# Half images at both ends of a gather-fed middle stage, and layer 3's first operands loaded during the gathers

## The chip, the core and the metric

The kernel runs on one core of one Trainium2 chip. The metric is the device time of one execution in microseconds (us). The core has five engines that run side by side, each in its own order: TensorE (PE; matmuls into PSUM, with the loading of weights shown apart as PEld), VectorE (DVE), ScalarE (ACT), GpSimd (POOL) and SyncE (SP, which starts most DMAs).

## The reference

Four layers are applied in turn to `x`, 8 images of 256 channels and 32 x 32 pixels. Layer 0 is an attention block and an MLP (256 to 1024 to 256, relu6), each after a batch norm over all images. Layer 1 is a bottleneck with a deformable 3 x 3 convolution, layer 2 a convolution of signs by signs with a batch norm over all images, layer 3 a second deformable block. What matters here, shortened:

```python
# end of layer 0
h = _relu6(jnp.einsum('bcn,hc->bhn', y2, w1) + bb1[None, :, None])
m = jnp.einsum('bhn,oh->bon', h, w2) + bb2[None, :, None]
xf = xf + m
# layer 1
h = jax.nn.relu(_bn(_conv1x1(x, w1), ...))            # 256 -> 64 channels
off = conv3x3(h, woff) + boff                          # 27 channels
o, mask = off[:, :18], jax.nn.sigmoid(off[:, 18:])     # 9 offsets (y, x) and 9 masks
samp = _bilinear(h, o_y + base_y, o_x + base_x) * mask # 4 cells around each place
h = einsum('bckhw,ock->bohw', samp, w2) + dcn_b
h = jax.nn.relu(_bn(h, ...))
x = jax.nn.relu(_bn(_conv1x1(h, w3), ...) + x)         # 64 -> 256 channels
# layer 2
y = conv3x3(sign(x), sign(weights)) * mean(abs(weights))
yn = (y - mean over all images) * rsqrt(var + EPS) * gamma + beta
x = yn + x
# layer 3
h = silu(bn(conv3x3(x, w_cv1)))                        # 256 -> 128 channels
...
```

The batch norm of layer 2 needs every image's convolution, so layer 3 can't begin before the last one is done.

## The kernel before

`x` lies in SBUF for the whole run: 128 partitions, 2 channel tiles `t`, 8 images `b`, 1024 pixels. A half image `h` is 512 pixels (16 rows), which is one bank of PSUM.

There are three stages. The first is layer 0's attention, to about 2706 us. The middle stage does the MLP of layer 0, layer 1 and layer 2, to about 3559 us; layer 3 follows. Only the middle stage and the first microseconds of layer 3 are changed.

The order of the middle stage comes from a planner, `Order` (L99 to L156). Every step is a "piece" with a key, an engine, a planned duration, a rank, the pieces it comes after, and the buffers that it takes and gives back: `pm` (2 banks) for the MLP, `po` (1), `pl` (3) for everything small, `pc` (1) for layer 2's convolutions; in SBUF `g` (3 gathered tiles), `idx`, `wts` and others. The planner puts next the piece that can start first by its plan, the lower rank first where two start together. It works when the program is built. The orders on PE, ACT, DVE and POOL are then fixed, and each engine runs its own strictly in order, whatever the real durations are.

An image goes through these pieces:

- MLP: `hidden` (L752), `relu6` (L757 on ACT, L759 on DVE), `mlp_out` (L765, 16 passes per half image and tile of channels), `mlp_add` (L769).
- `reduced` (L814) makes 64 channels; the two halves lie in the two halves of the partitions, so their matmuls can run paired. `reduced_relu` (L821) writes them twice into the bordered `h1`, as they are and shifted by one pixel.
- `table` (L827) transposes `h1` into 9 chunks of 128 cells; `table_copy` (L833) and `table_write` (L840, L842) put them into HBM as a table whose rows hold the four corner cells of a place, 8 DMAs of 1.15 MB in all. These are the DMAs of SP.
- `offsets` (L850) is the 3 x 3 convolution that makes offsets and masks, `offsets_copy` (L857) brings it to SBUF, `places` (L864) transposes it, `places_mask` (L872) is the sigmoid, `places_cells` adds the grid (L877) and calls `corners` (L776 to L797): it makes the cells (L791), then the four weights with the mask (L795, L797); L880 makes the index.
- `gather` (L885): 9 indirect DMAs per 128 pixels, 72 per image, all started by POOL. `near_weights` (L894) and `sample` (L907, L911, on DVE) weigh and add the four corners.
- `turn` (L919, L922), `turn_copy` (L931, L933): the samples are transposed back. `contract` (L942) is the deformable convolution's product, 5 blocks by 2 halves; `contract_relu` (L946), `expand` (L952), `expand_add` (L958), `expand_relu` (L962) end layer 1, and `sign` (L965) writes the bordered signs.
- `convolve` (L972): 18 matmuls in bf16 per image, output tile `o` and half; `convolve_stats` (L979), `convolve_copy` (L983) and a DMA of the result as int16 to `acc_d` in HBM (L984).

The convolutions of image `b` are held back until the places of image `b + 4` (at most the last) are done:

```python
piece(("v", *k), "PE", 3.9, 100 * b + 330, [("x", b, 0), ("x", b, 1), ("p", min(b + 4, B - 1))], convolve, *k, take=[("pc", "pl")[b == B - 1]])
```

After the stage, `batch_norm` (L207 to L221) makes the scale and shift of layer 2. Layer 3 has an `Order` of its own. It begins with DMAs of its weights (L1070 is `wc`, the convolution's), with selection matrices (`spread_rows`, L1155 to L1161, transposed by PE through the `ps` banks), and for each image with `load` (L1165, from `acc_d`), `normed3` (L1170, ACT), `add_normed` (L1174, DVE), `border` (L1177, into `xpad`), `convolve3` (L1182) and `silu` (L1187).

## Time and profile before

| | us |
|---|---|
| median of 3 runs | 4257.02 (4256.65 to 4259.13) |
| the profiled execution's own time | 4256.73 |
| its span | 4254.9 |
| first and last start of a gather (L885) | 2791.43 and 3516.02 |
| one gather on POOL, median of 576 | 0.946 |
| a gather's data, issue to landing, median | 2.7 |
| end of layer 2's last convolution | 3555.43 |
| first convolution of layer 3 (L1182) | 3571.01 |
| PE, DVE, ACT, POOL busy in the span | 3972.3, 3026.9, 1858.0, 3313.3 |

All times in rows are from the start of the span. A line of the timeline is start, duration, engine, source line, operation, output and inputs, how many instructions it joins, and in brackets how long the engine had been idle and what ended that. "x16" of an f32 matmul counts passes: an f32 matmul shows two. A row of a window gives the busy time of each engine in that stretch, the granted clock of TensorE as a share of full speed, and the share of time in which the DMA engines were busy. A row of waits gives the waiting engine and line, what it waited for, the sum, the number and the longest.

### The profile page before, as it was taken

What the parts mean: (1) busy time and instruction counts of PE and PEld (TensorE: products, weight loads), DVE (VectorE), ACT (ScalarE), POOL (GpSimd) and SP (SyncE); (2) the same over time, 40 slices, a digit from 0 to 9 for tenths busy, and PEclk for the clock granted to TensorE, in tenths of its full rate; (3) what the DMA queues carried; (4) which work ended last, traced back from release to release, by engine and by line L of the source; (5) the groups of instructions that cost most, each with busy time, mean ns of one, the idle gap of its engine ahead of it and who ended that gap; (6) DMA issues with size and microseconds to landing.
All of it is one profiled execution on the core that took longest, in us unless ns stands there. A gap on an engine that the chain in (4) does not pass through costs nothing.

```text
span 4254.9 us, 60310 instructions
## 1 busy us (share of the span) xinstructions
PE 3972.3 (93%) x20975; PEld 1542.8 (36%) x20975; DVE 3026.9 (71%) x5147; ACT 1858.0 (44%) x3335; POOL 3313.3 (78%) x2023
## 2 busy tenths in 40 slices
PE   6999999999999999999999999898899978999976
PEld 2333333333333333333333333343343333444432
DVE  6767777777777767777677776567777774777665
ACT  2555545545545555555555555332232324443321
POOL 2888889889898898888888889357777771489767
PEclk8999999999999999999999999999999998999998
DMA  5212212212222222122222121134344442000000
GB/s 174 62 54 57 77 50 63 71 50 65 66 56 69 59 59 73 51 65 68 53 60 74 51 62 48 45 99 115 116 120 121 121 132 72 5 11 15 15 15 21
DMA packets 207225, 283.11 MB, mean 67 GB/s; under 512 B 87216, under 2 KB 117440, under 8 KB 206656
## 3 DMA queue, kind: packets, MB, share of 16 engines
q1 hardware_dynamic: 176352, 195.46, 16.2%
q0 software_dynamic: 28720, 77.90, 6.2%
q10 hardware_dynamic: 1840, 5.81, 0.4%
q8 instruction: 169, 2.77, 0.3%
q14 instruction: 144, 1.18, 0.1%
HBM read 181.07 MB, written 63.82 MB: 58 GB/s over the span
## 4 chain that ended last, share of the span: by engine, by line
PE 72%; DVE 13%; POOL 7%; issue 4%; DMA 3%; ACT 2%; SPq 0%; DVEq 0%; POOLq 0%; ACTq 0%
PE av L460 20%; PE pb L403 12%; PE sc L448 11%; PE pb L386 5%; PE pc L1182 5%; POOL g L885 5%; PE pb L534 3%; PE pa L1366 2%; PE pb L330 2%; PE pm L752 2%; PE po L765 2%; DMA g<-table,idx 2%; DVE pm L407 2%; PE pw L1355 2%; DVE r L491 1%
## 5 line engine op out<-in xcount | busy, mean ns | idle before, releaser
L470 POOL TENSOR_TENSOR esum<-esum,e 128x1024 f32<-128x1024 f32 x762 | 1809.0, 2407 | 55.1 <-ACT e L449 54.7
L407 DVE TENSOR_REDUCE pm<-pb 128x1 f32<-128x512 f32 x2016 | 1356.3, 685 | 656.1 <-PE pb L403 652.0
L449 ACT ACTIVATE e<-sc 128x512 f32<-128x512 f32 x2048 | 1056.5, 603 | 677.0 <-PE sc L448 665.7
L460 PE MATMUL av<-e,v 128*64 128x512 f32 x4096 | 1054.2, 593 | 0.0
L403 PE MATMUL pb<-sk,sq 128*64 128x512 bf16 x4032 | 773.2, 387 | 56.3 <-DVE x L542 23.5
L885 POOL DMA_INDIRECT g<-table,idx x576 | 550.4, 955 | 256.4 <-issue 159.0
L403 PEld LDWEIGHTS <-sq 128*64 128x64 bf16 x4032 | 266.7, 109 | 911.5 <-issue 887.0
L448 PE MATMUL sc<-q,k 32*128 32x512 f32 x4096 | 590.6, 641 | 0.0
L468 POOL TENSOR_TENSOR esum<-e 128x1024 f32<-128x1024 f32 x127 | 303.2, 2409 | 298.9 <-ACT e L449 298.9
L460 PEld LDWEIGHTS av<-e,v 128*64 128x64 f32 x4096 | 295.0, 137 | 208.1 <-issue 117.3
L1374 POOL TENSOR_TENSOR part<-part,pr 128x512 f32<-128x512 f32 x224 | 289.4, 1293 | 67.5 <-DVE pr L1360 56.2
L1360 DVE TENSOR_TENSOR pr<-pw,v 128x512 f32<-128x512 f32 x400 | 258.0, 683 | 105.7 <-PE pw L1355 61.3
L1182 PE MATMUL pc<-xpad,wc 128*128 128x512 f32 x576 | 279.0, 611 | 4.1 <-ACT h L1187 4.1
L448 PEld LDWEIGHTS sc<-q,k 32*128 32x128 f32 x4096 | 164.6, 183 | 229.8 <-issue 185.6
L534 PE MATMUL pb<-o,wp 128*64 128x512 f32 x1024 | 244.3, 596 | 1.4 <-DVE r L512 1.2
L752 PE MATMUL pm<-y,wide 128*128 128x512 f32 x512 | 237.9, 609 | 6.1 <-DVE y L726 5.7
L386 PE MATMUL pb<-wide,y 128*64 128x256 f32 x2048 | 241.8, 379 | 0.0
L765 PE MATMUL po<-hid,w 128*128 128x512 f32 x512 | 239.7, 615 | 1.8 <-DVE x L769 1.7
L491 DVE RECIPROCAL r<-r 128x128 f32<-128x128 f32 x252 | 237.1, 942 | 0.1
L390 ACT COPY v<-pb 128x512 f32<-128x512 f32 x128 | 74.9, 585 | 266.0 <-PE pb L386 266.0
L907 DVE TENSOR_TENSOR near_p<-g,near_p 128x320 f32<-128x320 f32 (+1 forms) x384 | 177.3, 462 | 13.2
L911 DVE TENSOR_TENSOR samp<-samp,near_p 128x320 f32<-128x320 f32 (+1 forms) x384 | 174.0, 453 | 13.2
(256 smaller groups left out, 3893.7 us busy)
## 6 DMA issues: line engine op xcount, KB each, us to landing
sq<-lev_d SPq DMA_DIRECT2D x512, 64.0 KB
r<-r SPq DMA_DIRECT2D x504, 64.0 KB
sk<-lev_d SPq DMA_DIRECT2D x496, 64.0 KB
lev_d<-lev SPq DMA_DIRECT2D x180, 128.0 KB
u_d<-u SPq DMA_DIRECT2D x60, 256.0 KB
g<-table,idx POOLq DMA_INDIRECT x576, 2.7
table<-v SPq DMA_DIRECT2D x32, 256.0 KB
out<-res SPq DMA_DIRECT2D x32, 256.0 KB
```

The costliest lines, as they stand in the source:

```text
L386: nc.tensor.matmul(ps[c * 64 : (c + 1) * 64, (mt % 2) * 256 : (mt % 2 + 1) * 256], ys[b][:, t, k0 : k0 + 64], wv[:, t, g * 256 : (g + 1) * ...
L403: nc.tensor.matmul(ps[c * 64 : (c + 1) * 64, :], sq[pair][:, c, q0 : q0 + 64], sk[pair][:, c, kh * HALF : (kh + 1) * HALF], start=True, st ...
L407: nc.vector.tensor_reduce(maxima[m][:, pair, qt, kh : kh + 1], ps, AX.X, ALU.max)
L448: nc.tensor.matmul(ps, k[r, kt * P : (kt + 1) * P], q[r, h * HALF : (h + 1) * HALF], start=True, stop=True)
L449: nc.scalar.activation(es[m, kt, j // 2][:, j % 2, :], ps, AF.Exp)
L460: nc.tensor.matmul(av[i * HD : (i + 1) * HD, :], vss[b, g][:, kt, j * HD : (j + 1) * HD], e[:, i, :], start=kt == 0, stop=kt == NT - 1,)
L470: eng.tensor_add(sums[m, pair], sums[m, pair], es.pop((m, kt, pair)))
L534: nc.tensor.matmul(ps[c * 64 : (c + 1) * 64, :], wp[:, 2 * g + i, o0 : o0 + 64], outs[(b, g, h), i], start=i == 0, stop=i == 1,)
L752: nc.tensor.matmul(ps, w1[:, t, i * P : (i + 1) * P], ys[b, h][:, t, :], start=t == 0, stop=t == 1)
L765: nc.tensor.matmul(pss["o", b, h, t], w2[:, j, t * P : (t + 1) * P], hids[b, h, j], start=j == 0, stop=j == 7)
L885: nc.gpsimd.indirect_dma_start(out=g[:, k, :], out_offset=None, in_=tables[b][:TR, :], in_offset=bass.IndirectOffsetOnAxis(ap=idxs[b][:, t ...
L1182: nc.tensor.matmul(S["c", b, h], wc[:, t, k, :], tap(xpads[t], k, H // 2, h * H // 2), start=t == k == 0, stop=t == 1 and k == 8,)
```

## The change

It does the following things.

1. For image 0, `reduced`, `reduced_relu` and `table` go by half images, the table in chunks 0 to 3 and 4 to 8, and it is written in two parts (8 and 4 DMAs instead of 8 in all). `corners` is split into `cells` and `corner_weights`, for every image: the index no longer comes after the weights, nor the addition of the grid (`places_add`) after the mask. These DVE pieces get a lower rank.
2. For the last image, `contract` to `sign` go by half images, the lower half's contraction in two pieces of 256 columns. `convolve_upper` makes the upper half's convolution in two steps: all that needs the upper half's signs alone (the three lower taps for 15 of the 16 rows), into the MLP's banks `pm`; then the three lower taps of row 15, 12 matmuls of 32 columns. Convolutions of images 3 to 6 wait for the last hidden layer's outputs instead of the last image's places.
3. `w2` moves into a buffer `kept` that outlives the stage. When the last `mlp_out` is done, layer 3's weights `wc` are loaded into the same bytes. Image 0's convolution result is loaded into the bytes of `w1` that hold the first input tile (`ac0`). Layer 3 plans the load of image 0 at zero time.
4. The two `size` tiles of layer 2's weights go into one buffer that is later `h2`, and `scale` has an earlier rank.

The program's second branch for layer 3, for offsets out of range, is adapted to 1 and 3; the trace before shows no instruction of that branch. The diff, cut to its core:

```diff
+    keep = ctx.enter_context(tc.tile_pool(name="keep", bufs=1))
+    kept = keep.tile([P, 18 * P], F32, name="kept")
+    wc = kept.rearrange("p (t k o) -> p t k o", t=2, k=9)
+    ac0 = wide[:, 0, :].bitcast(I16).rearrange("p (t n) -> p t n", t=2)
...
-        w2 = w.tile([P, 8, C], F32, name="w2")
+        w2 = kept[:, 0 : 8 * C].rearrange("p (t o) -> p t o", o=C)
...
-        def corners(pool, wpool, pos, mask, npts, order):
+        def cells(pool, pos, npts, order):
...
+            iy, ix = order
+            cell = pool.tile([P, NT, npts], F32, name="cell")
+            nc.vector.scalar_tensor_tensor(cell, low[:, :, :, iy], float(PW), low[:, :, :, ix], ALU.mult, ALU.add)
+            return cell, low, over
+
+        def corner_weights(pool, wpool, pos, low, over, mask, npts, order):
+
             hi = over
...
-            return cell, wts
+            return wts
...
+        def reduced(b, hs=(0, 1)):
+            if hs[0] == 0:
+                pss["r", b] = bank()
+            ps = pss["r", b]
             for t in range(2):
-                for h in range(2):
+                for h in hs:
...
+        def chunks(b, i):
+
+            m = 8 if b else 4
+            return (0, m) if i == 0 else (m, NCH)
...
+            c0, c1_ = chunks(b, i)
+            for c in range(c0, c1_):
...
+        def table_write(b, c0, c1_):
+
+            if c0 == 0:
+                tables[b] = dram.tile([NCH * P, 4 * CB], F32, name=f"table1_{b}")
...
+                if c0 == 0:
+                    nc.sync.dma_start(tables[b][0 : P - shift, cols], vs[b][shift:P, 0, :])
+                c = max(c0, 1)
+                body = tables[b][c * P - shift : c1_ * P - shift, cols]
+                nc.sync.dma_start(body.rearrange("(t p) c -> p t c", p=P), vs[b][:, c:c1_, :])
...
+        def places_add(b):
+            pos = pss["pos", b] = one.tile([P, NT, K2, 2], F32, name="pos")
             for i in range(2):
                 nc.vector.tensor_add(pos[:, i::2], turned(b, i)[:, :, 0:18].rearrange("p q (k i) -> p q k i", i=2), grid[:, i::2])
-            cell, wtss[b] = corners(one, sb, pos, pss.pop(("m", b)), K2, (0, 1))
+
+        def places_cells(b):
+            cell, low, over = cells(one, pss["pos", b], K2, (0, 1))
             idxs[b] = sb.tile([P, NT, K2], I32, name="idx")
             nc.vector.tensor_scalar_add(idxs[b], cell, float(PW + 1))
...
+        def places_weights(b):
+            wtss[b] = corner_weights(one, sb, pss.pop(("pos", b)), *pss.pop(("l", b)), pss.pop(("m", b)), K2, (0, 1))
...
+        def contract(b, hs=(0, 1), n0=0, n1=HALF):
+            st, st8 = sts[b]
...
+                    v = st[:, i, h * HALF + n0 : h * HALF + n1] if i < 4 else st8[r, n0:n1]
+                    nc.tensor.matmul(ps[h * CB : (h + 1) * CB, n0:n1], wd[r, i, :], v, start=i == 0, stop=i == 4)
...
+        def convolve_upper(b, o, rest):
+
+            if not rest:
+                pss["v", b, o, 0] = pm.tile([P, HALF], F32, name="pm")
+            rows = H // 2
+            taps = [(t, k) for t in range(2) for k in (range(6, 9) if rest else range(9))]
+            for n, (t, k) in enumerate(taps):
+                r0, r1 = (rows - 1, rows) if rest else (0, rows - (k > 5))
+                nc.tensor.matmul(
+                    pss["v", b, o, 0][:, r0 * W : r1 * W], ws[:, t, k, o * P : (o + 1) * P], tap(xbs[b % 2][:, t, :], k, r1 - r0, r0),
+                    start=bool(n == 0 and not rest), stop=bool(rest and n == len(taps) - 1),
+                )
...
-        piece("scale", "PE", 1.0, 300, [("w", 0, 5), ("w", 1, 5)], scale_signs)
+        piece("scale", "PE", 1.0, 60, [("w", 0, 5), ("w", 1, 5)], scale_signs)
...
+            if b == 0:
+                for h in range(2):
+                    piece(("d", 0, h), "PE", 1.72, r, [("a", 0, h, t) for t in range(2)], reduced, 0, (h,), take=["pl"] * (1 - h))
+                    for i in range(2):
+                        piece(("dr", 0, i, h), "ACT", 0.8, r + i, [("d", 0, h), ("dr", 0, i - 1, h)], reduced_relu, 0, i, (h,), give=["pl"] * (h * i))
+                ready = [[("dr", 0, 0, 0)], [("dr", 0, 0, 1)]], [("dr", 0, 1, 0), ("dr", 0, 1, 1)]
+            else:
+                piece(("d", b), "PE", 2.0, r, [("a", b, h, t) for t, h in halves], reduced, b, take=["pl"])
+                piece(("d", b, 0), "ACT", 1.6, r, [("d", b), *old], reduced_relu, b, 0)
+                piece(("d", b, 1), "ACT", 1.6, r + 1, [("d", b, 0)], reduced_relu, b, 1, give=["pl"])
+                ready = [[("d", b, 0)]] * 2, [("d", b, 1)]
...
-                piece(("t", b, i), "PE", (0.9, 0.15)[i], r + 2, [("d", b, 0)], table, b, i, take=["pl"])
-                piece(("tc", b, i), "ACT", (0.6, 0.22)[i], r + 2, [("t", b, i), ("tw", b - 1), ("tc", b, i - 1)], table_copy, b, i, give=["pl"])
-            piece(("tw", b), "SP", 4.0, r, [("tc", b, 0), ("tc", b, 1)], table_write, b, lag=3.0)
-            piece(("f", b), "PE", 4.3, r + 3, [("d", b, 1)], offsets, b, take=["pl"])
+                piece(("t", b, i), "PE", ((0.9, 0.15) if b else (0.4, 0.5))[i], r + 2, ready[0][i], table, b, i, take=["pl"])
+                tw = [("tw", b - 1, 0), ("tw", b - 1, 1)]
+                piece(("tc", b, i), "ACT", (0.6, 0.22)[i], r + 2, [("t", b, i), *tw, ("tc", b, i - 1)], table_copy, b, i, give=["pl"])
+            if b == 0:
+                for i in range(2):
+                    piece(("tw", b, i), "SP", (4.0, 2.0)[i], r, [("tc", b, i)], table_write, b, *chunks(b, i), lag=3.0)
+            else:
+                piece(("tw", b, 1), "SP", 4.0, r, [("tc", b, 0), ("tc", b, 1)], table_write, b, 0, NCH, lag=3.0)
+            piece(("f", b), "PE", 3.2, r + 3 - 2 * (b == 0), ready[1], offsets, b, take=["pl"])
...
+            piece(("pa", b), "DVE", 0.75, r - 400, [("p", b), ("pw", b - 1)], places_add, b)
+            piece(("pm", b), "ACT", 0.5, r, [("pa", b)], places_mask, b, give=["pl"])
+            piece(("pc", b), "DVE", 2.3, r - 400, [("pa", b)], places_cells, b, take=["idx"])
+            piece(("pw", b), "DVE", 2.3, r - 400, [("pc", b), ("pm", b)], places_weights, b, take=["wts"])
...
+            if b == B - 1:
+                break
+            piece(("k", b), "PE", 4.4, -400, [("uc", b, u, j) for u in range(4) for j in range(3)], contract, b, take=["pl"])
+            piece(("kr", b), "ACT", 0.8, -400, [("k", b), ("e", b - 1, 0), ("e", b - 1, 1), "scale"], contract_relu, b, give=["pl"])
             for t in range(2):
                 piece(("e", b, t), "PE", 1.2, -400, [("kr", b)], expand, b, t, take=["pl"] * 2)
                 piece(("ea", b, t), "DVE", 1.45, -300, [("e", b, t)], expand_add, b, t, give=["pl"] * 2)
                 piece(("er", b, t), "ACT", 1.15, -300, [("ea", b, t)], expand_relu, b, t)
-        for b in range(B):
+        b = B - 1
+        for h in range(2):
+            for i, us in enumerate(((2,), (3,)) if h else ((0, 1),)):
+                n0, n1 = (256 * i, 256 * i + 256) if h else (0, HALF)
+                after = [("uc", b, u, j) for u in us for j in range(3)] + ([("k", b, 0, 0)] if h else []) + ([("k", b, 1, 0)] if i else [])
+                piece(("k", b, h, i), "PE", 2.2 if h else 4.4, -400, after, contract, b, (h,), n0, n1, take=["pl"] * (1 - i))
+            piece(("kr", b, h), "ACT", 0.7, -400, [("k", b, h, h), ("e", b - 1, 0), ("e", b - 1, 1)], contract_relu, b, (h,), give=["pl"])
+            for t in range(2):
+                piece(("e", b, t, h), "PE", 0.86, -400, [("kr", b, h)], expand, b, t, (h,), take=["pl"])
+                piece(("ea", b, t, h), "DVE", 0.73, -300, [("e", b, t, h)], expand_add, b, t, (h,), give=["pl"])
+                piece(("er", b, t, h), "ACT", 0.6, -300, [("ea", b, t, h)], expand_relu, b, t, (h,))
+                piece(("x", b, t, h), "ACT", 0.6, -100, [("er", b, t, h)] + [("v", b - 2, o, h_) for o in range(2) for h_ in range(2)], sign, b, t, (h,))
+
+        for b in range(B - 1):
             for t in range(2):
                 piece(("x", b, t), "ACT", 1.05, -100, [("er", b, t)] + [("v", b - 2, o, h) for o, h in halves], sign, b, t)
             for o, h in halves:
                 k = b, o, h
-                piece(("v", *k), "PE", 3.9, 100 * b + 330, [("x", b, 0), ("x", b, 1), ("p", min(b + 4, B - 1))], convolve, *k, take=[("pc", "pl")[b == B - 1]])
+                piece(("v", *k), "PE", 3.9, 100 * b + 330, [("x", b, 0), ("x", b, 1), ("p", b + 4) if b < 3 else ("o", B - 1, 1, 1, 1)], convolve, *k, take=["pc"])
                 piece(("vs", *k), "DVE", 0.7, -500, [("v", *k)], convolve_stats, *k)
-                piece(("vc", *k), "ACT", 0.6, -300, [("vs", *k)], convolve_copy, *k, take=["ac"], give=[("pc", "pl")[b == B - 1]])
+                piece(("vc", *k), "ACT", 0.6, -300, [("vs", *k)], convolve_copy, *k, take=["ac"], give=["pc"])
                 piece(("vd", *k), "SP", 0.4, 0, [("vc", *k)], lambda: None, give=["ac"])
+        b = B - 1
+        for o in range(2):
+            piece(("vu", o), "PE", 3.9, 100 * b + 330, [("x", b, 0, 0), ("x", b, 1, 0), ("h", b, 1, 7)], convolve_upper, b, o, 0, take=["pm"])
+        for h in range(2):
+            for o in range(2):
+                k = b, o, h
+                r = -200 + 10 * h + o
+                if h:
+                    piece(("v", *k), "PE", 3.9, r, [("x", b, 0, 1), ("x", b, 1, 1), ("v", b, 1, 0)], convolve, *k, take=["pl"])
+                else:
+                    piece(("v", *k), "PE", 0.5, r, [("x", b, 0, 1), ("x", b, 1, 1), ("vu", o)], convolve_upper, b, o, 1)
+                piece(("vs", *k), "DVE", 0.7, -500, [("v", *k)], convolve_stats, *k)
+                piece(("vc", *k), "ACT", 0.6, -300, [("vs", *k)], convolve_copy, *k, take=["ac"], give=["pl" if h else "pm"])
+                piece(("vd", *k), "SP", 0.4, 0, [("vc", *k)], lambda: None, give=["ac"])
+
+        piece("wc", "SP", 0.5, 0, [("o", B - 1, 1, t, 1) for t in range(2)], nc.sync.dma_start, wc, d["l3_wcv1"].rearrange("(t p) k o -> p t k o", p=P))
+        piece("ac0", "SP", 0.5, 0, [("h", B - 1, 1, 7)] + [("vd", 0, o, h) for o, h in halves], nc.sync.dma_start, ac0, acc_d[0])
...
+            if b == 0:
+                S["ac", b, t] = ac0[:, t, :]
+                return
...
-                piece(("ld", b, t), "SP", 0.5, r, [], load, b, t, take=["ld"], lag=5.0)
+                piece(("ld", b, t), "SP", 0.5 if b else 0.0, r, [], load, b, t, take=["ld"], lag=5.0 if b else 0.0)
```

## The prediction

> **What bounds the kernel now.** I read the page first (TensorE busy 93% of the span, GpSimd 78%), then the stretch 2706 to 3640 us by windows, since the edits lie only there.
>
> Busy time by window: window, sum, then PE, PEld, DVE, ACT, POOL, the granted TensorE clock, DMA share and GB/s.
> ```profile
> 3336.00:3427.00 91.00, 77.11 (x295) 33.39 (x294) 67.59 (x155) 24.84 (x48) 69.04 (x73) 0.94 0.43 124
> 3427.00:3517.00 90.00, 67.45 (x282) 28.29 (x281) 61.66 (x130) 20.06 (x37) 68.06 (x72) 0.91 0.41 123
> 3517.00:3571.00 54.00, 36.68 (x152) 14.87 (x151) 22.69 (x77) 15.96 (x22) 8.03 (x8) 0.89 0.21 68
> 3571.00:3640.00 69.00, 65.65 (x166) 28.74 (x166) 38.52 (x57) 40.70 (x54) 0.00 (x0) 0.94 0.14 45
> ```
> The first two rows are gathering images: GpSimd starts 72 gathers in each, no engine is full. The waits of GpSimd from 2780 to 3530 say what paces it:
> ```profile
> POOL g L885 <- issue: 159.0, 522, 0.3
> POOL g L885 <- DVE hid L759: 81.5, 2, 81.2
> ```
> A gather takes 0.95 us and the next follows 0.30 later, 576 of them from 2791.43 to 3516.97, with no stall over 0.3 us after the first (which had idled 81.2). So here the time is: when the first gather starts, a fixed 725.5 us, and what follows the last. Work on other engines is free as long as the stream is fed. Rows three and four are what follows: the tail of layers 1 and 2, and layer 3's start, where TensorE is the bound again (65.65 of 69 us).
>
> The timeline before the first gather (start, duration, engine, line):
> ```profile
> 2764.09 7.13 PE L765 MATMUL po<-hid,w 128*128 128x512 f32 x16 [0.84 <-DVE x L769]
> 2772.88 1.94 PE L814 MATMUL pl<-x,c 128*64 128x512 f32 x8
> 2774.95 3.16 ACT L821 ACTIVATE h<-pl,twice 64x512 f32<-64x512 f32 x4 [1.28 <-PE pl L814]
> 2784.68 1.28 ACT L872 ACT_TABLE_LOAD   x1
> 2786.30 0.37 DVE L877 TENSOR_TENSOR pos<-pl,grid 128x72 f32<-128x72 f32 x2 [1.18 <-ACT mask L872]
> 2790.39 0.19 DVE L880 TENSOR_SCALAR idx<-cell 128x72 int32<-128x72 f32 x1
> 2791.43 1.07 POOL L885 DMA_INDIRECT g<-table,idx  x1 [81.21 <-DVE hid L759]
> ```
> It is one chain; the positions wait for the mask's table load, the indices for all weights. The timeline after the last gather:
> ```profile
> 3524.57 4.17 PE L972 MATMUL pc<-xb,ws 128*128 128x512 bf16 x18 [0.80 <-ACT ac L983]
> 3528.66 4.66 PE L942 MATMUL pl<-st,wd 128*64 128x512 f32 x20
> 3533.40 0.78 ACT L946 ACTIVATE h<-pl,twice 128x512 f32<-128x512 f32 x1 [3.26 <-PE pl L942]
> 3539.13 16.30 PE L972 MATMUL pl<-xb,ws 128*128 128x512 bf16 x72 [1.81 <-ACT xb L965]
> ...
> 3571.01 2.05 PE L1182 MATMUL pc<-xpad,wc 128*128 128x512 f32 x2
> 3573.07 16.08 PE L1182 MATMUL pc<-xpad,wc 128*128 128x512 f32 x34
> ```
> A convolution of another image stands ahead of the last contraction, then all 72 convolution matmuls wait for the last sign. Call G the issue of the last gather (3516.02) and C the end of the last convolution (3555.43): C is G+39.4.
>
> **Part 1, first image.** By halves, TensorE gets half 0's table transposes and reduction ahead of the last MLP output. Unpaired, a half's reduction is four passes at 0.43 us, 1.72 instead of half of 1.94; with four transposes (0.77/9 each, 0.35) it puts 2.07 us on that path, and the last add ends at 2774.1 instead of 2772.0. Only half 1 follows: reduction 1.72, two relus of 0.79 instead of four. The offsets (2.95) then start near 2778.7 instead of 2779.07, and the positions' transposes end near 2783.75 instead of 2784.15. The add of positions no longer waits for table load and mask: about 2783.9 instead of 2786.30, 2.4 gained. The indices leave the weights behind: from add to index 2.65 us instead of 4.28, 1.6 gained. First gather at 2786.55 + 0.85 (end of the index to the gather, as now) = 2787.4 against 2791.43: **4.0 us**. The weights (1.5 us, L795 and L797) now lie behind the index and beside the first gathers, whose data land 2.7 us after issue.
> The table is the limit close by. It is written in 12 DMAs instead of 8, the second part four of 160 KB. At the 155 GB/s that the queue ran in 2780 to 2788 this is 4.1 us from 2779.8, and with the landing near 2786, just ahead of the index. The Trainium skill, "DMA: Bandwidth & Descriptors", Anatomy of one DMA, speaks against more DMAs: about 2 us fixed for each. The trace: eight issues spanned 6.1 us and traffic ended 2.6 us after the last. If that stood in series for the four more, 8 us, the table would be there at 2794, part 1 would lose 2.6 and the sum would be 4242.8; in the trace eight lie over each other, so I take the rate. Ends: 2 gained (table late by 2) and 5.
>
> **Gathers, images 1 to 7.** 576 issues stay. The order of instructions puts three 18-matmul convolutions (4.17 each) ahead of the last image's positions on TensorE, whose indices are now ready at 3415.9 for a gather due near 3427.3. Also positions and indices move forward on VectorE relative to the samples: before image 6's index (from 0) the spare time was 1.4 us, now more. For the last image I estimate 3 to 4 us left of 11, with the 4-us earlier start taken off. I book 0, ends 0 and -6 (TensorE's work from the MLP to those positions, all matmuls at their rows' durations, is 642.7 us by the new order and 628.9 by the old; with all 13.8 uncovered, some 6 go beyond the spare time, since the images' other waits take up part).
> The convolution weights of layer 3 (1.18 MB) and its first input add DMA traffic to windows with a DMA share of 0.41: hidden, 0; if the gathers' landings rose by a us, the ring of three buffers covers it. The scale step, index-queue and buffer edits: 0, all inside windows where PE is idle 14 to 22 us of 90. On SP, nothing that a gather needs is queued behind the two new loads once the last table is written.
>
> **Part 2, last image.** After the last sample (G+6.0) come transposes and copies as now. The convolution of 4.17 plus its waits no longer stands before the contraction: it starts near G+7.5 instead of G+12.6, 5.1 gained. Its last piece is 10 passes of 256 columns, half of 4.66: 2.3 gained, less 0.2 for its start. Expand and sign of one half, with 9 to 12 small matmuls before the stats (1.1 to 1.7 us at a weight load of 0.10 to 0.14 each), cost 0.75 more than they save. The 36 upper matmuls, 36 x 0.2264 = 8.15, are taken ahead into TensorE's idle time before G. Together 14.5: C = G+24.9.
> Here the clock weighs against. The rows: this same 18-matmul convolution took 4.17 us after waits of 0.8 to 1.8, but 6.19 at 3489.53 after a transpose that had ended 3.87 us of idleness, and the granted clock fell to 0.50 at 2692 after a gap of 2.49. The Trainium skill, "TensorE: Matmul & The Clock Gate", Part 1, states half rate after about one idle window of 3.4 us, free-running. My tail leaves TensorE idle some 2.6 us (expand ends G+12.7, last sign G+15.3), shorter than the page's window, so by the page no loss (sum 4235.2); by the rows the 36 last matmuls would lose 2.0 (4237.2). The free-running window leaves it open, I take 1: **13.5 us**, ends 10 and 16.
>
> **Part 3, layer 3's start.** With image 0's input resident, the plan puts normalization (L1170, L1174) ahead of most selection pieces (L1159): the first bordered image is ready near C+10.95, the first convolution at C+11.2 instead of C+15.6. 4.4 gained. But six of the ten selection transposes then stand between the convolution's matmuls: 6 x 0.2 to 0.47, less the one there now, 1.4 lost. TensorE starts at half clock both ways: the rows are 2.05 for two passes, then 16.08 for 34, with granted clock 0.50 until 3573 and 0.66 to 3577; the 11-us gap keeps that loss of about 2.3 where it is. By the page it is 3.4 us of half-rate work, 1.7 lost, also in both. **3.0 us**, ends 1 and 6. The load of the weights itself is worth little: issued at 3558.70, it was in before xpad was. The rest of layer 3 has the same order on every engine, with TensorE at 542 of 614 us, so the shift carries to the end.
>
> **Sum.** 4.0 + 0 + 13.5 + 3.0 = 20.5. The profiled execution took 4256.73 (span 4254.9 and 1.8 around it), 0.3 under the median of 4257.02: 4236.2.
>
> **The rivals.**
> 1. A part is lost: the last image's positions stall the gathers by up to 6, or the table is late by 2, or the selection pieces hold the convolution (2 instead of 4.4). For it: 11 us of spare time against 12.5 us of moved matmuls. Against: TensorE idles 14 us in that very window. Loss 6: 4242.
> 2. The clock stays full and layer 3 starts earlier than I think: 16 + 6 + 5 = 27, 4230.
> 3. Slower: VectorE stops. It runs in order, so if the add of the last image's positions stands there waiting for TensorE, the samples behind it wait too, g's three buffers stay full and GpSimd stops. Price: each us beyond the 3.5 spare is one on the gather stream. It decides from 20.5 + 3.5 = 24 us of lateness; at 36, 32.5 are lost against 20.5 gained, 4268.7. Against it: TensorE's moved and added work is 13.8 us, so 36 would need its own waits to grow by 22.
> 4. The change does not do what it says: the tail's gain goes back because the final convolution isn't bound by the last sign (the upper 36 matmuls fall after G instead of before). Price 8.15: 4244. The order shows them all ahead of the last contraction, which is against.
>
> **How the numbers follow.** Forecast 62%, rival 1 21%, rival 2 9%, rival 4 4%, rival 3 4%. Range 4228 to 4246: bounds 27 and 13 of the three parts, with a stall of 3 on the lower. 0.2%, 8.5 us, is what a measurement here can tell from no change. A gain under 8.5 needs two losses at once or half of rival 3: 3%; slower by over 0.2% only rival 3's far end: 2%.
>
> **What would show it.** First gather at 2787 to 2788; no wait over 0.5 us on GpSimd later, above all at 72 gathers from the end; last convolution 25 to 27 us after the last gather, with 36 matmuls in 8.2 (10 if cold); first silu of layer 3 near C+31 instead of C+33.8. The forecast is wrong if a gap stands before the last image's gathers, or if C stays beyond G+30.

## The result, and the profile after

The changed kernel takes 4238.32 us (median of 6 runs, 4236.48 to 4241.13) against 4257.21 (6 runs, 4255.68 to 4259.13): 18.9 us less, a ratio of 0.9955 with a 95% interval of 0.9942 to 0.9968. Forecast were 4236.2, a gain of 20.5, in a range of 4228 to 4246. The profiled execution took 4237.45; its span is 4235.2 against 4254.9, 19.7 less. The new line numbers are `hidden` L758, `mlp_out` L771, `gather` L913, `convolve` L1006, `convolve_upper` L1020, `convolve3` L1277; `places_add` is L899 and the index L904.

The 19.7 us can be followed by five marks in both traces:

| stretch | before | after | gain | forecast |
|---|---|---|---|---|
| span's start to the first gather | 2791.43 | 2788.62 | 2.8 | 4.0 |
| first to last gather | 724.59 | 724.26 | 0.3 | 0 |
| last gather (G) to the end of layer 2's last convolution (C) | 39.41 | 28.97 | 10.4 | 13.5 |
| C to layer 3's first silu table load | 33.80 | 29.25 | 4.6 | 3.0 |
| from there to the end | 665.67 | 664.10 | 1.6 | 0 |

The last row is no effect of the change that these runs could show: it lies anywhere from 664.1 to 665.6 in the kernels below, which all have the same code there.

The waits of GpSimd from 2780 to 3530 after the change (waiting engine and line, releaser, sum, times, longest):

```profile
POOL g L913 <- issue: 159.9, 525, 0.3
POOL g L913 <- DVE wm L806: 79.3, 3, 78.7
```

The stream of gathers has no stall, as before. VectorE's L806 is named for the first gather only because it ended last by the records; the index is what counts. The timeline ahead of that gather (start, duration, engine, line, operation, then idle time and what ended it):

```profile
2767.01 7.13 PE L771 MATMUL po<-hid,kept 128*128 128x512 f32 x16 [0.84 <-DVE x L775]
...
2775.79 1.93 PE L827 MATMUL pl<-x,c 128*64 128x512 f32 x4
...
2785.13 0.37 DVE L899 TENSOR_TENSOR pos<-pl,grid 128x72 f32<-128x72 f32 x2 [4.31 <-PE pl L886]
...
2785.62 1.28 ACT L894 ACT_TABLE_LOAD   x1
...
2787.57 0.20 DVE L904 TENSOR_SCALAR idx<-cell 128x72 int32<-128x72 f32 x1
...
2788.62 1.07 POOL L913 DMA_INDIRECT g<-table,idx  x1 [78.65 <-DVE wm L806]
```

The last MLP output starts 2.9 us later than before (2764.09), the positions no longer wait for the table load, and from their add to the index's end it is 2.6 us. The tail:

```profile
3514.51 0.41 PE L947 MATMUL pl<-ident,samp 128*128 128x128 f32 x2 [1.45 <-DVE samp L939]
...
3518.79 0.69 PE L947 MATMUL pl<-ident,samp 128*128 128x128 f32 x2 [3.87 <-DVE samp L939]
...
3520.16 4.72 PE L972 MATMUL pl<-st,wd 128*64 128x256 f32 x10 [0.25 <-ACT st L959]
3524.91 0.77 ACT L978 ACTIVATE h<-pl,twice 64x512 f32<-64x512 f32 x1 [4.42 <-PE pl L972]
3525.74 3.78 PE L984 MATMUL pl<-h,c 64*128 64x512 f32 x4 [0.86 <-ACT h L978]
...
3531.78 0.40 PE L1020 MATMUL pm<-xb,ws 128*128 128x32 bf16 x9 [1.47 <-ACT xb L999]
3532.02 9.83 PE L1006 MATMUL pl<-xb,ws 128*128 128x512 bf16 x36
```

The reader should see three durations here. Ten contraction passes of 256 columns take 4.72 us, as long as the twenty of 512 columns before, which ran in pairs (4.66). Four expand passes take 3.78, where eight took 3.09. And 36 convolution matmuls take 9.83, where 72 took 16.30. TensorE's windows say why (busy time, PEclk, DMA share, GB/s):

```profile
3509.00:3513.00 4.00, 4.00 (x20) 1.00 0.46 131
3513.00:3516.00 3.00, 0.47 (x3) 1.00 0.32 93
3516.00:3519.00 3.00, 0.21 (x1) 0.91 0.00 0
3519.00:3522.00 3.00, 2.75 (x9) 0.50 0.00 0
3522.00:3525.00 3.00, 2.87 (x7) 0.50 0.00 0
3525.00:3528.00 3.00, 2.26 (x3) 0.50 0.00 0
3528.00:3531.00 3.00, 1.76 (x5) 0.50 0.07 25
3531.00:3534.00 3.00, 2.22 (x14) 0.50 0.70 238
3534.00:3537.00 3.00, 3.00 (x11) 0.75 0.26 87
```

For 17 us the granted clock is half, from 3518.46 to 3535.52. It falls in the 3.87 us in which TensorE waits for the last sample. These 17.07 us are five times 3.41. In all 14 traces shown or named here every spell of half and of full clock lasts a whole multiple of 3.41 us (the last one is cut by the end of the span), so the clock changes from one window of 3.41 us to the next and not at the wait itself. The start of layer 3 has such a spell too (first convolution, first silu's table load, and the stretch between, before and after):

```profile
3553.54 4.04 PE L1277 MATMUL pc<-xpad,kept 128*128 128x512 f32 x6
3571.10 1.28 ACT L1282 ACT_TABLE_LOAD   x1 [0.75 <-PE pc L1277]
```

```profile
3571.01:3589.23 18.22, 18.14 (x38) 0.87 0.29 98
3553.54:3571.10 17.56, 17.56 (x43) 0.93 0.25 76
```

### The profile page after: what moved, and what is told of

Its sections match the earlier page's. It is cut to its first block, busy times and chain, and to the rows that moved or that the text cites. A ratio compares the mean times of both kernels' runs of the same rounds, so it can differ in the third digit from the quotient of the medians.

```text
span 4235.2 us, 60371 instructions
## 1 busy us (share of the span) xinstructions
PE 3972.8 (94%) x20997; PEld 1543.9 (36%) x20997; DVE 3026.4 (71%) x5147; ACT 1862.2 (44%) x3340; POOL 3312.4 (78%) x2023
## 4 chain that ended last, share of the span: by engine, by line
PE 69%; DVE 13%; POOL 8%; issue 5%; DMA 3%; ACT 1%; SPq 0%; DVEq 0%; POOLq 0%; ACTq 0%
PE av L460 20%; PE pb L403 12%; PE sc L448 11%; POOL g L913 6%; PE pb L386 5%; PE pc L1277 5%; PE pb L534 3%; PE pa L1461 2%; DMA g<-table,idx 2%; PE pb L330 2%; DVE pm L407 2%; PE pw L1450 2%; PE pm L758 2%; DVE r L491 1%; PE pb L481 1%
## 5 line engine op out<-in xcount | busy, mean ns | idle before, releaser
L403 PE MATMUL pb<-sk,sq 128*64 128x512 bf16 x4032 | 772.8, 387 | 56.7 <-DVE x L542 23.5
L913 POOL DMA_INDIRECT g<-table,idx x576 | 550.1, 955 | 253.8 <-issue 159.9
L1277 PE MATMUL pc<-xpad,kept 128*128 128x512 f32 x576 | 276.7, 606 | 4.0 <-ACT h L1282 4.0
L758 PE MATMUL pm<-y,wide 128*128 128x512 f32 x512 | 235.6, 606 | 6.1 <-DVE y L732 5.7
L771 PE MATMUL po<-hid,kept 128*128 128x512 f32 x512 | 239.8, 617 | 1.5 <-DVE x L775 1.4
```

The lines of the kernel that those rows point to most:

```text
L403: nc.tensor.matmul(ps[c * 64 : (c + 1) * 64, :], sq[pair][:, c, q0 : q0 + 64], sk[pair][:, c, kh * HALF : (kh + 1) * HALF], start=True, st ...
L758: nc.tensor.matmul(ps, w1[:, t, i * P : (i + 1) * P], ys[b, h][:, t, :], start=t == 0, stop=t == 1)
L913: nc.gpsimd.indirect_dma_start(out=g[:, k, :], out_offset=None, in_=tables[b][:TR, :], in_offset=bass.IndirectOffsetOnAxis(ap=idxs[b][:, t ...
L1277: nc.tensor.matmul(S["c", b, h], wc[:, t, k, :], tap(xpads[t], k, H // 2, h * H // 2), start=t == k == 0, stop=t == 1 and k == 8,)
```

## The experiments

Each kernel is the changed one with the edit shown, but for `before_order`. Totals come with few runs, so most verdicts rest on a stretch of the trace. Where TensorE never waits in a stretch, its work at half clock took twice as long, so half of the time at half clock can be taken off, and what is left compares. The first four kernels ran beside a kernel before of 4258.98; `no_halves` took 4235.54, `scale_later` 4235.80 and `hold_convs` 4238.92, one run each.

**no_halves.** Image 0 is taken whole again.

```diff
-            m = 8 if b else 4
+            m = 8
-            if b == 0:      # reduced, reduced_relu, table_write by halves
+            if b < 0:
```

> The changed kernel, with image 0 taken whole again (reduction, relus, table in 8 DMAs); only the split of index and weights and the add ahead of the mask stay. Theory: the index sets the first gather and the halves bring nothing, since the 2.6 us that they put ahead of the last MLP output eat what they save: first gather near 2787.7, 1 us before the changed kernel's 2788.62. Rival: the table sets it once the index is early; eight DMAs issued to 2786 with traffic to 2788.6, as in the kernel before, then hold the first gather at 2789 to 2790. The prediction's own step (halves worth 0.0 to 0.4 by its terms, 2.07 paid for 2.4 saved) says 2788. Everything behind the first gather shifts with it, within 1 us in the total.

Two lines of the timeline:

```profile
2785.16 0.20 DVE L904 TENSOR_SCALAR idx<-cell 128x72 int32<-128x72 f32 x1
...
2788.46 1.07 POOL L913 DMA_INDIRECT g<-table,idx  x1 [80.13 <-DVE hid L765]
```

The index is there at 2785.36, but the gather starts 3.10 us later instead of 0.85. The last table DMA was issued up to 2784.5 and the DMA engines were busy to about 2786.6; the trace names no other cause, so the table is taken to have held it. The stage had begun 1.64 us earlier in this execution (first hidden matmul 2708.75 instead of 2710.39). Counted from there the first gather comes after 79.71, against 78.23 changed and 80.78 before. In these three the stage began with 5.7, 5.9 and 4.9 us at half clock; with half of that taken off, 76.84, 75.26 and 78.33 are left. The rival is right: the split of index and weights alone earns 1.5, and the halves 1.6 more, all of it through the table, for which the index alone would have been too early.

This kernel shows something else in its tail, where its instructions and their order are the changed kernel's. G to C is 27.09 here, against 28.97:

```profile
3525.13 2.11 PE L984 MATMUL pl<-h,c 64*128 64x512 f32 x4 [0.86 <-ACT h L978]
```

```profile
3523.46:3526.85 3.39, 2.53 (x7) 1.00 0.00 0
```

The clock fell here as well, at 3516.62, but was full for one window of 3.41 us when the expand ran, which took 2.11 instead of 3.78. `scale_later` has the same tail too, and 28.25. A tail without added matmuls so takes 27.1 to 29.0.

**scale_later.** The sum of the weights' sizes is put behind image 0's places.

```diff
-        piece("scale", "PE", 1.0, 60, [("w", 0, 5), ("w", 1, 5)], scale_signs)
+            if b == 0:      # in the loop, behind ("p", 0)
+                piece("scale", "PE", 1.0, 60, [("w", 0, 5), ("w", 1, 5), ("p", 0)], scale_signs)
```

> The changed kernel, with the eight small matmuls that sum the sign weights' sizes (0.8 us of TensorE, ahead of image 0's last MLP output in both kernels) put after image 0's places. Theory (one chain of TensorE sets the first gather): 2788.62 goes to 2787.8. Rival (the table's DMAs are late as well): it stays within 0.3. Nothing else moves; total 0 to 1 us shorter.

The first gather is at 2787.66, 77.53 after the first hidden matmul. But that stage began with 4.6 us at half clock here and 5.9 in the changed kernel's trace; with half of it taken off, 75.23 and 75.26 are left. `warm_tail` and `hold_convs`, whose code is the changed kernel's up to there, have 77.56 and 77.61, both 75.25 without that half. So nothing was gained: the last add did come 0.9 earlier than in those two (62.2 after the stage's start instead of 63.1 and 63.2), but the sum now stood in TensorE's order behind the places, and its result (L753) in VectorE's ahead of the positions' add, which began 1.3 us after the places were begun instead of 0.4. One queue's delay had become another's.

**warm_tail.** Matmuls of constants, read by nobody, fill TensorE's idle time.

```diff
+        def warm(n):
+            ps = po.tile([P, HALF], F32, name="po")
+            for i in range(n):
+                nc.tensor.matmul(ps, ws[:, 0, 0, 0:P], ws[:, 0, 0:2, :].rearrange("p k o -> p (k o)"), start=True, stop=True)
+        piece(("warm", 0), "PE", 0.0, -450, [("u", b, 3, 0), ("vu", 1)], warm, 14)
+        piece(("warm", 1), "PE", 0.0, -450, [("e", b, 1, 1)], warm, 5)
```

> The changed kernel, plus 14 matmuls of constants whose results nobody reads, in TensorE's 3.9 us idle ahead of the last image's last transposes, and 5 more after the last expand. Theory (the tail lost its 4 us against the prediction to the clock, which fell to half in that idle time): the contraction of ten 256-column passes takes 2.4 instead of 4.72, the four expand passes 1.8 instead of 3.78, the last 36 convolution matmuls 8.2 instead of 9.83, and from the last gather's issue to the end of the last convolution it is 23.5 to 25 instead of 29.0; total 4 to 5.5 us shorter than the changed kernel. Rival (the tail waits for ScalarE and VectorE, the clock hides behind it): under 1.5 us. Second rival (work added in TensorE's order is in the way): longer.

G to C is 27.42 instead of the 23.5 to 25 expected, and the median 4235.99 (4 runs; 0.9949, 0.9932 to 0.9965). Only the last 36 matmuls came out at full clock (8.17); contraction and expand were 4.71 and 3.78. The 14 had run too early: the last four transposes are one piece, two of them ready and two waiting for the last sample, and the planner put the 14 ahead of the piece. A gap of 2.63 us was left inside it, and the clock fell in it, at 3516.28. The tail's 27.42 lies within what it takes with no such matmuls, so nothing is shown to be gained.

**hold_convs.** The convolutions of images 3 to 6 wait for the last image's places again.

```diff
-("p", b + 4) if b < 3 else ("o", B - 1, 1, 1, 1)
+("p", min(b + 4, B - 1))
```

> The changed kernel, with the convolutions of images 3 to 6 held back again for the last image's places. Two of them then stand around the last transposes, as in the kernel before. Theory (clock): they keep TensorE at full clock, so the contraction takes 2.4 to 2.6 us and the last 36 matmuls 8.2; but one of 4.2 us stands ahead of the contraction, so the tail from last gather to last convolution is 25 to 29, no longer than the changed kernel's 29.0. Rival (moving them out of the way was worth the predicted 5.1): 32 to 34. For the gathers: no stall before the last image either way; its index is ready some 5 to 12 us earlier than in the changed kernel against the gather.

```profile
3518.43 4.17 PE L1006 MATMUL pc<-xb,ws 128*128 128x512 bf16 x18 [0.61 <-ACT ac L1030]
3522.52 2.51 PE L972 MATMUL pl<-st,wd 128*64 128x256 f32 x10
3525.90 1.98 PE L984 MATMUL pl<-h,c 64*128 64x512 f32 x4 [0.86 <-ACT h L978]
```

The convolution is in the way again and the contraction takes 2.51, the expand 1.98; the clock was full until 3530.22. G to C is 29.12, against 27.1 to 29.0 without the convolutions. Moving them away had bought between nothing and 2 us in the tail, not 5.1: they paid for most of their place by the clock. Of the gathers' spare time: the last image's index was ready at 3407.67, 14.7 us ahead of its first gather (71 gathers of 1.25 before the last); in the changed kernel at 3420.94, 3.2 ahead, and in the kernel before 11.2.

**warm_turn, upper_late, load_planned, before_order** ran on another chip, where the kernel before took 4590.67 us. Between first and last gather single engines stood still there for up to 36 us at a time. A line of ScalarE's timeline in `warm_turn`:

```profile
3501.26 0.78 ACT L980 ACTIVATE h<-pl,twice 128x512 f32<-128x512 f32 x1 [27.44 <-remote]
```

Its input was ready 20 us before (L974 had ended at 3480.91); TensorE had nothing to do from 3483.26 on, but GpSimd went on gathering until 3496.73. So ScalarE stopped first here, and the others ran dry behind it: PE, DVE, ACT and POOL were all idle at once for 6.4 us at most, not up to 28 as the expectation of `warm_turn_2` has it. ScalarE's waits of this kind sum to 335 us in this trace, which is 342 longer than that of `warm_turn_2`. No queue or engine of the profile shows what it waited for, and the gathers stretched to 1025 to 1058 us in all four kernels. Their totals (4575 to 4598), and their tails, say nothing on the change; the start of layer 3 lies behind the stalls and can be read. The two tails were run again.

**load_planned.** `load` for image 0 is planned at 0.5 us and a lag of 5 again; the data are in SBUF as in the changed kernel.

> The changed kernel, with image 0's load planned at 0.5 us and a lag of 5 again, though the data are in SBUF; only the planned order at layer 3's start changes. Theory (the order of normalization against selection pieces is the gain): end of the last convolution to first silu table load goes from 29.25 to 33 to 34, total 4 to 5 longer. Rival (the gain is the data's being there): it stays at 29 to 30.

**before_order.** The kernel before, with this one edit:

```diff
-                piece(("ld", b, t), "SP", 0.5, r, [], load, b, t, take=["ld"], lag=5.0)
+                piece(("ld", b, t), "SP", 0.5 if b else 0.0, r, [], load, b, t, take=["ld"], lag=5.0 if b else 0.0)
```

> The kernel before, with image 0's load planned at zero time and nothing else changed: the load from HBM and layer 3's weights (1.18 MB, issued 3.3 us after the last convolution) stay. Theory (order alone): from the last convolution's end to the first silu table load 29.3 to 30.5 instead of 33.8, total 3 to 4.5 us shorter than the kernel before. Rival (the early order needs the early weights): the first convolution matmul of layer 3, possible near 11.7 us after, waits for the weights, which at the 225 GB/s that the DMA queue reached in short stretches land 9 us after at the earliest and at 155 near 11; silu 31 to 34.

The first silu's table load in `load_planned`, and then in `before_order`; C was 3889.12 and 3878.19:

```profile
3923.91 1.28 ACT L1282 ACT_TABLE_LOAD   x1 [5.20 <-PE pc L1277]
```

```profile
3907.81 1.28 ACT L1187 ACT_TABLE_LOAD   x1 [0.75 <-PE pc L1182]
```

That is 34.79 us after C with the data there and the old plan, and 29.62 with the data and weights loaded as before and the new plan. The order is the gain; the early loads bring nothing that these runs can show. Layer 3's first convolution even started sooner without them: 10.6 us after C in `before_order`, 11.4 to 11.7 with the same order and the early loads, and under the old plan 15.6 before and 16.9 in `load_planned`. What costs this microsecond stays open.

**warm_turn, warm_turn_2.** The 14 matmuls stand inside the last piece of transposes; the five behind the expand stay:

```diff
                     nc.tensor.transpose(ps[:, i * P : (i + 1) * P], sf[:, j, i * P : (i + 1) * P], ident)
+                    if (b, u, j, i) == (B - 1, 3, 1, 1):
+                        warm(14)
```

> The changed kernel, plus 14 matmuls of constants that nobody reads, this time between the second and third of the last image's last four transposes (L947), which is where the 3.9 us of idle TensorE lie; and 5 after the last expand as in warm_tail. There the 14 had run ahead of the first two transposes, an idle gap of 2.6 us was left, and the clock fell at 3516 all the same; only the last 36 matmuls (8.17 instead of 9.83) came out at full clock, 1.55 us gained. Theory (the idle gap sets the clock, the clock the tail): no window at 0.50 from the last gather to the last convolution; contraction 2.5 instead of 4.72, expand 2.0 instead of 3.78; last gather's issue to the end of the last convolution 23.4 to 24.5 instead of 29.0. Rival (the clock falls for low activity, not for one gap): contraction at 4.7 again, 27 or more.

`warm_turn` is one of the four above (4584.69, 0.9993 of a kernel before that stalled alike). The same kernel again:

> The same kernel as warm_turn, which had run on a chip where all engines stood still for up to 28 us at a time in the middle stage (the kernel before took 4590 there), so that its tail could not be read. Expected as there: no clock of 0.50 between last gather and last convolution; contraction 2.5, expand 2.0, last gather's issue to end of last convolution 23.4 to 24.5 instead of 29.0, total 4 to 5.5 us shorter than the changed kernel. Rival (low activity cools it, not one gap): contraction 4.7, 27 or more.

```profile
3512.02 3.19 PE L1030 MATMUL po<-ws 128*128 128x512 bf16 x14
3516.22 0.44 PE L947 MATMUL pl<-ident,samp 128*128 128x128 f32 x2 [1.02 <-DVE samp L939]
...
3517.33 2.51 PE L974 MATMUL pl<-st,wd 128*64 128x256 f32 x10 [0.46 <-ACT st L961]
3520.71 2.17 PE L986 MATMUL pl<-h,c 64*128 64x512 f32 x4 [0.86 <-ACT h L980]
...
3525.61 8.24 PE L1008 MATMUL pl<-xb,ws 128*128 128x512 bf16 x36
```

The gap is 1.02 us, contraction and expand are short again, and G to C is 23.69 instead of 27.1 to 29.0: 3.4 to 5.3 us for work that computes nothing. The median is 4233.02 (4 runs) against a kernel before of 4255.67, 0.9946 (0.9931 to 0.9961). One part of the expectation failed: the clock was at half for one window.

```profile
3518.97:3522.36 3.39, 2.53 (x8) 1.00 0.00 0
3522.38:3525.77 3.39, 3.23 (x19) 0.50 0.51 164
```

In the window ahead of it TensorE had worked for 2.5 of 3.4 us, and its longest gap there was 0.86. So a long gap is not needed; the rival, that low activity brings the clock down, is not refuted by this run, since the 14 matmuls both close the gap and add work.

**upper_late, upper_late_2.** The upper half's 36 matmuls are convolved whole, behind the signs, instead of ahead of the last contraction.

```diff
-        for o in range(2):
-            piece(("vu", o), "PE", 3.9, 100 * b + 330, [("x", b, 0, 0), ("x", b, 1, 0), ("h", b, 1, 7)], convolve_upper, b, o, 0, take=["pm"])
-                    piece(("v", *k), "PE", 0.5, r, [("x", b, 0, 1), ("x", b, 1, 1), ("vu", o)], convolve_upper, b, o, 1)
+                    piece(("v", *k), "PE", 3.9, r, [("x", b, 0, 1), ("x", b, 1, 1)], convolve_whole, b, o, take=["pm"])
```

> The changed kernel, with the last image's upper half convolved whole and in the tail, behind both halves' signs; its contraction to sign still go by halves. Theory (36 matmuls of 0.2264 us are moved off the path, 0.6 of small ones paid): from the last gather's issue to the end of the last convolution 36 to 37 instead of 29.0, total 7 to 8 us longer than the changed kernel. Rival (the early 36 are what leaves TensorE idle at the wrong moment, or something else holds the end): under 5 longer.

The first of the two stalled as told (4598.32). The second:

> The same kernel as upper_late, for the same reason. Expected: last gather's issue to the end of the last convolution 36 to 37 instead of 29.0; rival under 34.

```profile
3525.59 3.78 PE L984 MATMUL pl<-h,c 64*128 64x512 f32 x4 [0.86 <-ACT h L978]
3529.30 9.39 PE L1020 MATMUL pm<-xb,ws 128*128 128x512 bf16 x36
3538.53 8.17 PE L1006 MATMUL pl<-xb,ws 128*128 128x512 bf16 x36
```

G to C is 34.09, the total 4243.81 (one run), between the two expectations. Taking 8.15 us of work off the path is worth 5.1 against the changed kernel's trace, whose clock was at half over contraction and expand as it is here, and up to 7.0 against 27.09. With it in the tail TensorE goes on at once after the expand, since the first of these matmuls need only the upper half's signs. Without it TensorE has nothing there but twelve small matmuls, nine of which need the last sign, and starts its last 36 behind them, at 3532.02, 2.5 us after its expand has ended (3529.52). Neither expectation had this wait in it. That is 2.5 of the 3.0 by which 5.1 falls short of 8.15. Most of the rest is the clock: here the upper 36 warmed it for the last 36, which took 8.17 instead of 9.83, and paid 1.2 for it themselves.

**all_together.** `warm_turn` and `scale_later`, with 30 more matmuls of constants behind the last convolution and six short ones between layer 3's first selection transposes.

> The changed kernel, with the constants' matmuls of warm_turn, with 30 more behind the last convolution and six short ones between the first selection transposes of layer 3 (so that its first convolution starts at full clock), and with the sizes' sum behind image 0's places as in scale_later. Theory (clock and chain add up): first gather 0.7 to 0.9 earlier against the stage's start, tail 23.4 to 24.5, last convolution to first silu 26.5 to 27.5 instead of 29.25; together 7 to 9 us shorter than the changed kernel, 4229 to 4232 where that has 4238. Rival (layer 3's first convolutions wait for normalization, not for TensorE): silu 29 as before, 4232 to 4234.

4233.41 (5 runs; 0.9947, 0.9934 to 0.9961). The first six passes of layer 3's convolution took 2.74 instead of 4.04, so at full clock, but they began 14.8 us after C instead of 11.7. The first gather (78.21 after the stage's start) gained nothing, as in `scale_later`. The tail took 25.16, longer than in `warm_turn_2`: the clock had fallen 3.3 us ahead of G, the 14 matmuls took 5.59 instead of 3.19, and the last transposes stood behind them. VectorE's timeline:

```profile
3541.59 1.16 DVE L1197 TENSOR_SCALAR center<-ident 128x128 f32<-128x128 f32 x1 [2.71 <-PE po L1030]
```

The 30 matmuls read the middle stage's weights, and layer 3's tiles are put into that memory: its first writes waited for them. The silu came 31.04 after C, later than in the changed kernel.

**warm_and_scale.** Without the 30, and with four short ones.

> The changed kernel with the constants' matmuls of warm_turn_2, the sizes' sum behind image 0's places as in scale_later, and four short matmuls of constants between layer 3's first selection transposes; the 30 behind the last convolution are gone, because in all_together layer 3's first writes into freed memory waited for them (VectorE 2.7 us). Theory (clock): tail 23.5 to 24.5, first convolution of layer 3 11.7 to 12.3 after the last one of layer 2, at full clock (six passes in 2.7 instead of 4.0 to 4.9), first silu 27.5 to 28.5 instead of 29.3 to 30.1; 6 to 8 us shorter than the changed kernel, so 0.9935 to 0.9945 of the kernel before. Rival (the short matmuls do not lift the clock in 4.5 us): silu 30, 0.9945 to 0.995.

4233.44 (5 runs) against 4257.17: 0.9942, 0.9928 to 0.9956. The rival is right: six passes took 4.06 and the silu came 29.95 after C. The short matmuls filled TensorE from 7.2 us after C nearly to the convolution at 12.4, and the clock was still half. Its tail was 23.92. It and `warm_turn_2` have the lowest medians: 23.7 and 22.7 us less than the kernel before beside them, where the changed kernel has 18.9. But the intervals of the ratios overlap, and the single runs of `no_halves` and `scale_later`, with no added matmuls, are 23.4 and 23.2 below theirs. A gain in the total is not shown; the stretch G to C carries this, with 23.7, 23.9 and 25.2 in three traces with the 14 matmuls in place and 27.1, 28.2 and 29.0 in three without.

## Why the prediction was right or wrong

**The bound was right.** The gather stream kept its 724 us, and the gain came from its two ends and layer 3's start, as forecast. The last image's index was the tie that was named, with 3.2 us left of 11.2 (3 to 4 estimated), and no stall followed.

**Part 1: 4.0 forecast, 2.8 measured,** and 3.1 with the half-clock time at the stage's start taken off in both (78.33 less 75.26). Two terms were small. The halves put 2.5 us ahead of the last MLP output, not 2.07 (63.1 from the stage's start to the last add in `warm_tail`, against 60.6 before, where the first passes took as long to 0.2 us). From that add's end to the gather it took 13.7 us, not the 13.3 of the working. The table was the limit close by, as the prediction said, and `no_halves` shows which way: the halves are worth their price because the table is ready earlier, not because the positions are; of those the prediction had them gain 0.4. More DMAs did not cost 2 us each: the four of the second part were issued from 2780.70 to 2782.84 and the DMA engines were done by 2785. The 2 us that the prediction took from the Trainium skill's page "DMA: Bandwidth & Descriptors", Anatomy of one DMA, stand there for DMAs that GpSimd starts, and these are SyncE's.

**Part 2: 13.5 forecast, 10.4 measured, 10.4 to 12.3 over the three traces of this tail. The step that failed is the clock's price, 1 us.** The prediction looked for idle TensorE behind the expand (2.6 us) and found the clock's fall a toss-up there. The gap that did it in the changed kernel's trace was an earlier one, 3.87 us ahead of the last two transposes, and it came from the step itself: "5.1 gained" took away the convolution that had filled this time, and the halved contraction, "2.3 gained", then ran at half clock in the time that the whole one had needed. Filled with matmuls of constants, the tail is 23.7 and 23.9 us, near the G+24.9 of the sum before the clock; so the clock cost 3.2 to 5.3, not 1. How much differs from one execution to the next: tails of 27.1, 28.2 and 29.0 had 12.4, 14.1 and 17.1 us at half clock after G+5. `hold_convs` shows the same from the other side. The Trainium skill's page "TensorE: Matmul & The Clock Gate", Part 1, names an idle window of about 3.4 us; the changed kernel's trace agrees with it (no work from 3515.04 to 3518.46, then half clock). But in `warm_tail` the clock fell after a window with 1.2 us of work in it, in `warm_turn_2` after one with 2.5, and there the measurement decides.

For the 36 upper matmuls the sum had 8.15, and `upper_late_2` has 5.1 to 7.0. This does not show the term wrong, since that kernel is not the one before: it has the halves, behind which part of these matmuls hides. One reading was wrong: the 72 matmuls before did not wait for the last sign, but began at 3539.13 on the first tile's (done at 3539.07), while the second's began at 3540.14.

**Part 3: 3.0 forecast, 4.6 measured** in this pair, 3.0 to 4.7 over the traces of layer-3 starts with this order and no added matmuls between (silu 29.1 to 30.8 after C, against 33.80). The first convolution starts 3.9 earlier, not 4.4. From its first pass to the silu's table load it is 17.6 us, 18.2 before, of which 2.5 and 4.7 were at half clock; with half of that taken off, 16.3 and 15.9 are left. So the selection transposes between the passes cost 0.45, where 1.4 had been taken off, and the clock gave 1.1, where the prediction had the same loss in both. That was luck: ten traces with this order, `before_order` among them, have 16.31 to 16.33 without the half, and between 2.5 and 5.5 us at half clock, from which the spread of the silu comes. That the loads themselves are worth little was right: `before_order` has the gain without them.

**The sum** is 0.8 over the profile's 19.7: parts 1 and 2 were 1.2 and 3.1 too high, part 3 and the gathers 1.6 and 0.3 too low, and 1.6 came from the spread of the end of layer 3. Errors of both signs met, so that the total came out better than its terms was luck.

## What to carry to other kernels

Before work is moved off a path, look at what it kept busy: a matmul in the way may be what holds TensorE's clock, and ten unpaired passes at half clock took as long as twenty paired ones at full. Compare two traces of a stretch only with its time at half clock beside them: the same tail took 27.1 to 29.0 us here, and layer 3's start 17.6 to 19.1. A wait that is cut in one queue pays only as far as the next operand allows; here the index was early and the table was not. When a plan gives a load a long lag, try the plan's order alone before building the earlier load.

## What the runs showed of the hardware

- TensorE's clock was at half or at full, and every spell of either lasted a whole multiple of 3.41 us. The longest gap did not decide alone. The clock fell in a gap of 2.63 us in `warm_tail` and after a window whose longest gap was 0.86 in `warm_turn_2`; the wait of 2.10 us at layer 3's first silu brought it down in `no_halves` and not in the changed kernel. What the windows count is not shown.
- After a fall it took 17 us to come back in the changed kernel, with windows in which TensorE was busy for 83 to 88% by the trace and stayed at half; over 5 us of short f32 matmuls did not lift it in `warm_and_scale`.
- On one chip of those that were used, both kernels lost 330 to 340 us in the gathering stage to stalls with no releaser in the trace, and the gain with them: 0.9993 (0.998 to 1.0005) for `warm_turn`. ScalarE's stalls make up nearly all of it there (335 us). What stops it stays open.
- The first 20 passes of the middle stage took 11.1 to 11.8 us from one execution to the next, and 8.80 in all 14 traces with half of their time at half clock (4.5 to 6.0) taken off. So starts of a stage are compared from its own first instruction, and without that half.
